# A backward scan of maxima in one instruction, or in pieces of 128 columns

## The chip, the cores and the metric

The kernel runs on one core of a Trainium2 chip. The core has five engines with a queue of instructions each: TensorE (PE in the profile; its weight loads are PEld), VectorE (DVE), ScalarE (ACT), GpSimd (POOL) and SyncE (SP). They work side by side and wait for each other through semaphores, each engine in the order of its own queue. The metric is the device time of one execution in microseconds.

## The reference, cut to what matters

Four graph layers run one after the other over the same graph of 12500 nodes and 212500 edges, sorted by the node that they end in (`dst`): two graph attention layers (GAT), a transformer convolution with 8 heads, a message layer that takes a maximum, and a layer that takes a mean. The first three hold a softmax over the edges of each node. From the transformer convolution:

```python
alpha = jnp.einsum('ehd,ehd->eh', q[dst], k[src]) / jnp.float32(np.sqrt(HD))
m = jax.ops.segment_max(alpha, dst, num_segments=n)
ex = jnp.exp(alpha - m[dst])
den = jax.ops.segment_sum(ex, dst, num_segments=n) + 1e-16
a = ex / den[dst]
agg = jax.ops.segment_sum(a[:, :, None] * v[src], dst, num_segments=n)
```

The GAT layers do the same with one logit for each edge, `leaky_relu(alpha_src[src] + alpha_dst[dst], 0.2)`. What matters here is `m[dst]`: each edge needs the maximum over all edges of its node, in each head.

## The kernel before

The edges lie in chunks of 128, one edge for each partition; a tile is 17 chunks (`U`), and there are 98 tiles (`T`). A layer is a pass over the tiles (`edge_pass`): gat1, gat2, attn, max and sum follow each other. A pass is written out as a calendar of rounds: the parts of a tile's work (`load`, `gather`, `e1`, `chain`, `e2`, `batch`, `ends`) are generators that are put at fixed rounds, and in each round every live generator issues its next few instructions. This settles the order of each engine's queue; nothing reorders it later. Parts of three or four tiles are interleaved.

For a tile, POOL gathers the rows of the source nodes, one indirect DMA for each chunk (L1245), into 17 or 18 buffers of three chunks (`g`). `e1` makes the logits: with matmuls against one-hot matrices (L1528, tile `ex`) in the GAT passes, with L1646, L1651 and L1652 in attn. `chain` makes the maxima and the exponentials. `e2` multiplies the gathered rows with the exponentials (L1580 in the GAT passes, L1675 in attn). That is the last reader of a gather buffer, and POOL's next gather into that buffer waits for it. `batch` sums the products into the nodes of a tile (L1300, one-hot matrix `sef` or `se` from L1291 or L1134), and `ends` finishes the nodes: in attn with a dense network, of which L880 is the last matmul and L713 the statistics on its result.

The maxima are made in `chain` by `node_max`. The logits are transposed (L1463, tile `lt`), so that the edges run along the free axis: one row of 128 columns for each chunk and head. `k` is the number of neighbouring chunks that one row holds one after the other, with one more at each end for the edges that a node has there: k = 1 and 17 rows in the GAT passes, k = 3 and 6 x 8 = 48 rows in attn. The list `n0` holds 0 where an edge has the node of the edge before it and -1e30 where a new node starts. A forward scan (L1451, `fw`) goes through k + 2 chunks: state = max(state + n0, logit). At the last edge of a node it has the node's maximum. A backward scan (L1470, `bw`) over the last k + 1 chunks carries that value back to the node's other edges: 256 columns in the GAT passes, 512 in attn. The forward scan works in stretches of four chunks, since it reads PSUM banks; in attn it is one of 512 columns and one of 128, which starts from the last value of the first. Then PE transposes k chunks of `bw` back (L1475, tile `pbx`), DVE subtracts (L1554 to L1561, or L1664), and ACT takes the exponential (L1563, or L1666). In gat2, DVE's L832 stands between the scan and L1554; SP's store L833 waits for it, and the loads of `n0` (L1415) and `gt` (L1307) come behind that store in SP's queue.

Of the kernel before, what the change touches and what calls it, by code (L numbers as in the profile page):

```python
# [14 lines left out]
ALU = mybir.AluOpType  # L15
# [6 lines left out]
P = 128  # L22
# [43 lines left out]
def gnn_kernel(ctx, tc, a, out):  # L66
    nc = tc.nc
    V, S, GP, PE, SY = nc.vector, nc.scalar, nc.gpsimd, nc.tensor, nc.sync
# [140 lines left out]
    k = WB * P + 1  # L209
    GP.iota(rd_i[0:1, :k], pattern=[[1, k]], base=-k, channel_multiplier=0)  # L210
    k = E - (U * P * (T - 1) - WB * P - 1)
    GP.iota(rd_i[96:, k:], pattern=[[1, EW + 2 - k]], base=4 * NP, channel_multiplier=0)
    GP.memset(dd_i[0:1, 0:1], -1)
    k = E - (P - 1) * RC * P
# [915 lines left out]
    def by4(tag, name):  # L1130
        return psum([P, 512], tag, name).rearrange("p (j e) -> p j e", e=P)
# [309 lines left out]
    def node_max(pool, lg, n0, k, h, pb):  # L1441


        g = -(-U // k)
        r, w = g * h, (k + 2) * P
        fw = pool.tile([r, w], F32, name="fw")
        todo = None

        def forward():
            s0, n, lt = todo  # L1450
            V.tensor_tensor_scan(fw[:, s0 * P:(s0 + n) * P], n0[:, s0 * P:(s0 + n) * P],  # L1451
                                 lt[:r, :n, :].rearrange("p j e -> p (j e)"),
                                 fw[:, s0 * P - 1:s0 * P] if s0 else 0.0,
                                 op0=ALU.add, op1=ALU.max)

        for s0 in range(0, k + 2, 4):
            n = min(4, k + 2 - s0)
            if todo:
                forward()
            lt = by4("pm", "lt")  # L1460
            for s in range(s0, s0 + n):
                g0 = (s - 1) // k + 1
                PE.transpose(lt[:r, s - s0, :],  # L1463
                             lg[:, (s - 1) % k, g0:g0 + g, :].rearrange("p g h -> p (g h)"), ident)
            todo = s0, n, lt
            yield
        forward()
        yield
        bw = pool.tile([r, w - P], F32, name="bw")
        V.tensor_tensor_scan(bw[:, ::-1], n0[:, P + 1:w + 1][:, ::-1], fw[:, P:][:, ::-1], 0.0,  # L1470
                             op0=ALU.add, op1=ALU.max)
        yield
        pb = pb[:, :k * r].rearrange("p (s r) -> p s r", s=k)
        for s in range(k):
            PE.transpose(pb[:, s, :], bw[:, s * P:(s + 1) * P], ident[:r, :r])  # L1475
        yield
        return pb.rearrange("p s (g h) -> p s g h", g=g)
# [11 lines left out]
    class gat(Pass):  # L1489
# [54 lines left out]
        def chain(self, u):  # L1544
            pool, c = self.pool, self.c
            n = chunks_of(u)
            am, lg = self.am[u], self.lg[u]
            neighbours(self.lg, u, 1)
            yield
            ps_ = psum([P, 512], "ex", "pbx")  # L1550
            pb = yield from node_max(pool, lg, self.n0[u], 1, 1, ps_)

            ml = pool.tile([P, 2, U], F32, name="ml")
            V.tensor_tensor(ml[:, 0, :n], am[:, :n, 0], pb[:, 0, :n, 0], ALU.add)  # L1554
            V.tensor_tensor(ml[:, 1, :n], am[:, :n, 0], lg[:, 0, 1:1 + n, 0], ALU.add)
            V.scalar_tensor_tensor(ml[:, :, :n], ml[:, :, :n], 0.2, ml[:, :, :n],
                                   op0=ALU.mult, op1=ALU.max)
            V.tensor_max(ml[:, 0, :n], ml[:, 0, :n], am[:, :n, 1])
            d = pool.tile([P, 2, U], F32, name="d")
            V.tensor_tensor(d[:, 0, :n], ml[:, 1, :n], ml[:, 0, :n], ALU.subtract)  # L1560
            V.tensor_tensor(d[:, 1, :n], am[:, :n, 1], ml[:, 0, :n], ALU.subtract)  # L1561
            p = self.p[u] = ps_[:, 256:256 + 2 * U].rearrange("p (i c) -> p i c", i=2)
            S.activation(p[:, :, :n], d[:, :, :n], AF.Exp)  # L1563
            yield

            lo = self.lo[u] = pool.tile([P, U, 2], F32, name="lo")
            fi = FIRST[:, u * U:u * U + n]
            V.tensor_mul(lo[:, :n, 0], p[:, 1, :n], fi)
            S.copy(lo[:, :n, 1], fi)
            yield  # L1570
# [40 lines left out]
    class attn(Pass):  # L1611
# [43 lines left out]
        def chain(self, u):  # L1655
            pool = self.pool
            lg = self.lg[u]
            neighbours(self.lg, u, 3)
            yield
            ps_ = psum([P, 512], "ex", "pbx")  # L1660
            pb = yield from node_max(pool, lg, self.n0[u], 3, H, ps_)
            g = -(-U // 3)
            d = pool.tile([P, 3, g, H], F32, name="d")
            V.tensor_tensor(d, lg[:, :, 1:g + 1, :], pb, ALU.subtract)  # L1664
            p = self.p[u] = ps_[:, 256:256 + 3 * g * H].rearrange("p (g s h) -> p g s h", s=3, h=H)
            S.activation(p, d.rearrange("p s g h -> p g s h"), AF.Exp)  # L1666
            yield
# [245 lines left out]
```

## Time and profile before

| what | value |
|---|---|
| time, median of 4 runs | 14943.55 us (14927.04 to 14957.47) |
| profiled execution | 14959.69 us, its span 14958.0 us |
| instructions in the profile | 149840 |
| backward scans L1470 | 294: 196 of 17x256, 98 of 48x512 |
| granted TensorE clock, 2000 to 3000 us (gat1) | 0.50 |
| granted TensorE clock, 5200 to 6300 us (gat2) | 0.59 |
| granted TensorE clock, 7300 to 8300 us (attn) | 0.77 |

The profile is one execution on the chip. A line of the timeline has the start and the duration in us, the engine, the line of the kernel, the operation, the tile it writes and those it reads, their shape, and in brackets how long the engine was idle before and what ended that. A line of the groups has the shape, the count, the busy time in us, the mean duration of one in ns and the idle time before them. "Remote" stands for a wait that the profile can't put down to an instruction, "issue" for idle time without such a wait.

### The profile page before, as it was taken

What the parts mean: (1) busy time and instruction counts of PE and PEld (TensorE: products, weight loads), DVE (VectorE), ACT (ScalarE), POOL (GpSimd) and SP (SyncE); (2) the same over time, 40 slices, a digit from 0 to 9 for tenths busy, and PEclk for the clock granted to TensorE, in tenths of its full rate; (3) what the DMA queues carried; (4) which work ended last, traced back from release to release, by engine and by line L of the source; (5) the groups of instructions that cost most, each with busy time, mean ns of one, the idle gap of its engine ahead of it and who ended that gap; (6) DMA issues with size and microseconds to landing.
All of it is one profiled execution on the core that took longest, in us unless ns stands there. A gap on an engine that the chain in (4) does not pass through costs nothing. (4 is left out here: it accounts for less than half of the span.)

```text
span 14958.0 us, 149840 instructions
## 1 busy us (share of the span) xinstructions
PE 7844.6 (52%) x47184; PEld 6088.4 (41%) x47185; DVE 4582.6 (31%) x15188; ACT 4642.6 (31%) x13171; POOL 7855.1 (53%) x8330
## 2 busy tenths in 40 slices
PE   4444444444555555455555555568887785333333
PEld 2222222223444444344444444446665563333333
DVE  4333333332333333344444444423333331000000
ACT  4444444442333333233333333323333332111111
POOL 3445445545555555444444444455555555666665
PEclk5555555555555555677777777767777776666666
DMA  4211111112233322333333333322222222222222
GB/s 112 57 52 50 49 47 50 49 53 80 86 86 86 86 85 85 92 97 97 101 96 97 98 101 97 94 64 75 75 73 75 76 75 59 67 69 70 69 68 68
DMA packets 759391, 1146.93 MB, mean 77 GB/s; under 512 B 224152, under 2 KB 491623, under 8 KB 758479
## 3 DMA queue, kind: packets, MB, share of 16 engines
q0 software_dynamic: 292368, 610.29, 16.0%
q1 hardware_dynamic: 465536, 526.83, 11.1%
q8 instruction: 374, 6.13, 0.2%
q14 instruction: 441, 3.61, 0.1%
q10 hardware_dynamic: 672, 0.07, 0.0%
HBM read 964.76 MB, written 171.69 MB: 76 GB/s over the span
## 5 line engine op out<-in xcount | busy, mean ns | idle before, releaser
L1245 POOL DMA_INDIRECT g<-t,IDX x3322 | 3138.2, 945 | 2947.4 <-issue 1943.9
L1300 PE MATMUL acc<-xf,sef 128*128 128x131 f32 (+2 forms) x13458 | 2752.1, 367 | 1093.5 <-issue 352.5
L1300 PEld LDWEIGHTS acc<-xf,sef 128*128 128x128 f32 x13458 | 2395.2, 263 | 1300.7 <-issue 448.7
L1245 POOL DMA_INDIRECT g<-tkv,IDX x1661 | 1569.7, 945 | 2005.4 <-DVE xf L1675 1490.1
L1245 POOL DMA_INDIRECT g<-ts__84,IDX x1661 | 1567.5, 944 | 1151.6 <-issue 422.2
L1245 POOL DMA_INDIRECT g<-th,IDX x1661 | 1567.8, 944 | 936.7 <-issue 517.7
L1300 PE MATMUL acc<-g,sef 128*128 128x129 f32 x4486 | 883.5, 376 | 1569.8 <-ACT sef L1291 1083.1
L1300 PEld LDWEIGHTS acc<-g,sef 128*128 128x128 f32 x4486 | 818.9, 282 | 1634.4 <-ACT sef L1291 1128.6
L1291 ACT CAST sef<-se 128x512 f32<-128x512 fp8e4 (+1 forms) x1755 | 1030.0, 599 | 1197.0 <-remote 957.0
L1528 PE MATMUL ex<-ADX,st 128*128 128x6 bf16 x4486 | 362.5, 175 | 1216.7 <-ACT st L1134 494.9
L1716 DVE TENSOR_TENSOR_SCAN fm<-n,fm,pg 128x384 f32<-128x384 bf16 (+1 forms) x585 | 567.0, 969 | 1351.9 <-PE pg L1713 557.8
L1315 DVE COPY_PREDICATED r<-FLAG,gt 128x129 f32<-128x129 int32 (+2 forms) x490 | 144.9, 296 | 2568.4 <-ACT r L1321 1913.2
L1528 PEld LDWEIGHTS <-st 128*128 128x128 fp8e4 x4486 | 332.2, 115 | 1436.4 <-issue 747.9
L1651 DVE TENSOR_TENSOR g<-qe,g 128x384 f32<-128x384 f32 x586 | 310.4, 530 | 1601.7 <-remote 1305.5
L1726 ACT COPY xf<-pt_f 128x384 f32<-128x384 f32 x586 | 270.2, 461 | 1271.0 <-PE pt_f L1722 389.2
L1141 PE MATMUL pm_st<-fe,NF 5*128 5x384 bf16 (+2 forms) x877 | 381.5, 458 | 528.8 <-ACT se L1134 477.6
L1646 PE MATMUL qe<-q,st 128*128 128x128 bf16 x6729 | 586.5, 249 | 62.9 <-DVE g L1651 35.8
L1149 PE MATMUL pm_se<-NF,fa 5*128 5x128 bf16 x4486 | 618.8, 278 | 0.0
L1300 PEld LDWEIGHTS <-se 128*128 128x128 fp8e4 x2243 | 238.3, 130 | 910.6 <-issue 555.8
L1134 ACT ACTIVATE se<-pm_se,ones 128x512 fp8e4<-128x512 f32 (+1 forms) x585 | 390.8, 668 | 694.4 <-remote 461.4
L1300 PE MATMUL acc<-xs,se 128*128 128x201 bf16 x2243 | 483.6, 368 | 197.9 <-ACT se L1134 134.7
L1134 ACT ACTIVATE st<-pm_st,ones 128x384 fp8e4<-128x384 f32 (+2 forms) x877 | 468.6, 534 | 365.5 <-PE pm_st L1141 199.6
(1099 smaller groups left out, 12510.7 us busy)
## 6 DMA issues: line engine op xcount, KB each, us to landing
se<-se_d SPq DMA_DIRECT2D x294, 368.0 KB
st<-st_d SPq DMA_DIRECT2D x196, 368.0 KB
g<-t,IDX POOLq DMA_INDIRECT x3322
n<-first_d SPq DMA_DIRECT2D x97, 544.0 KB
st_d<-st SPq DMA_DIRECT2D x98, 368.0 KB
se_d<-se SPq DMA_DIRECT2D x98, 368.0 KB
g<-tkv,IDX POOLq DMA_INDIRECT x1661
g<-ts__84,IDX POOLq DMA_INDIRECT x1661
```

Of the source, the lines that this page charges most:

```text
L1134: S.activation(out, pm[:, :out.shape[1], :], AF.Relu, scale=-1.0, bias=ones[:, 0:1], saturate=False)
L1141: PE.matmul(pm[:, :n, :].rearrange("p j e -> p (j e)"), NF, f[:, c * P:(c + n) * P], start=True, stop=True)
L1149: PE.matmul(pm[:, j, :], f[:, (c + j) * P:(c + j + 1) * P], NF, start=True, stop=True)
L1245: GP.indirect_dma_start(out=g[:, j, :], out_offset=None, in_=self.table, in_offset=bass.IndirectOffsetOnAxis(ap=IDX[:, k:k + 1], axis=0))
L1291: S.copy(se, self.se[t][:, at, :])
L1300: PE.matmul(acc[:, :m], se[:, j, :], x[:, i, :], start=(b == 0 and j == 0), stop=(b == n - 1 and j == len(ws) - 1))
L1315: V.copy_predicated(r[:, :w], FLAG[:, t:t + 1].to_broadcast([P, w]), self.gt[:, :w])
L1528: PE.matmul(ex[:, 6 * k:6 * k + 6], st, ADX[:, t, :, :].rearrange("p s v -> p (s v)"), start=(first and c0 == 0), stop=(stop and c0 + n - ...
L1646: PE.matmul(qe[0][:, k - c0, :], st, self.q[t][:, s * D:(s + 1) * D], start=(first and s == 0), stop=(stop and s == 2))
L1651: V.tensor_mul(k, qe[0][:, :n, :], k)
L1716: V.tensor_tensor_scan(fm[:, :m, :].rearrange("p j e -> p (j e)"), self.n0[u][:, cols], pg, self.prev, op0=ALU.add, op1=ALU.max)
L1726: S.copy(ft[:, :m, :D], pt[:, :m, :])
```

## The change

The backward scan is split into k + 1 instructions of 128 columns each, made from the last chunk to the first. The first of them starts from 0.0 as the whole scan did; each other one starts from the first column of the piece behind it, which is the last value that the backward scan made there, read as a value for each partition. What is computed is the same. There are two instructions in place of one in the GAT passes and four in attn, so 294 scans become 784. The line numbers behind it move by four; the new scan is L1472.

```diff
         bw = pool.tile([r, w - P], F32, name="bw")
-        V.tensor_tensor_scan(bw[:, ::-1], n0[:, P + 1:w + 1][:, ::-1], fw[:, P:][:, ::-1], 0.0,
-                             op0=ALU.add, op1=ALU.max)
+        for s in reversed(range(k + 1)):
+            at = slice(s * P, (s + 1) * P)
+            V.tensor_tensor_scan(bw[:, at][:, ::-1], n0[:, P + 1:][:, at][:, ::-1],
+                                 fw[:, P:][:, at][:, ::-1],
+                                 bw[:, (s + 1) * P:(s + 1) * P + 1] if s < k else 0.0,
+                                 op0=ALU.add, op1=ALU.max)
         yield
```

## The prediction

> **What bounds the kernel now.** I read the engine row of the page first.
>
> ```profile
> PE 7844.6 (52%) x47184; PEld 6088.4 (41%) x47185; DVE 4582.6 (31%) x15188; ACT 4642.6 (31%) x13171; POOL 7855.1 (53%) x8330
> ```
>
> No engine is full, so waits set the time, not work. The change touches DVE only, and DVE is idle for 69% of the span; an average says nothing here. The second view is the groups of instructions with different shapes kept apart, for the backward scan (L1470) and its nearest relative, the forward scan (L1451).
>
> ```profile
> L1451 DVE TENSOR_TENSOR_SCAN fw<-n,lt 17x384 f32<-17x384 bf16 x196 | 184.6, 942 | 718.2 <-PE lt L1463 333.1 <-remote 314.5 <-PE ex L1528 70.5
> L1470 DVE TENSOR_TENSOR_SCAN bw<-n,fw 17x256 f32<-17x256 bf16 x196 | 133.0, 678 | 6.6
> L1470 DVE TENSOR_TENSOR_SCAN bw<-n,fw 48x512 f32<-48x512 bf16 x98 | 119.2, 1217 | 3.3
> L1451 DVE TENSOR_TENSOR_SCAN fw<-n,lt 48x512 f32<-48x512 bf16 x98 | 118.7, 1211 | 140.1 <-PE lt L1463 130.0 <-remote 10.1
> L1451 DVE TENSOR_TENSOR_SCAN fw<-n,fw,lt 48x128 f32<-48x128 bf16 x98 | 45.3, 463 | 0.2 <-PE lt L1463 0.2
> ```
>
> The number after the busy time is the mean of one in ns. The last row is what the change makes: 128 columns that start from a value in SBUF. The third view is the timeline, one tile in each of the three passes that call the scan. Pass gat1 (200 to 3350 us), a tile:
>
> ```profile
> 2038.69 0.94 POOL L1245 DMA_INDIRECT g<-t,IDX  x1 [0.30 <-issue]
> ...
> 2046.07 0.94 DVE L1451 TENSOR_TENSOR_SCAN fw<-n,lt 17x384 f32<-17x384 bf16 x1 [3.55 <-PE lt L1463]
> ...
> 2047.04 0.68 DVE L1470 TENSOR_TENSOR_SCAN bw<-n,fw 17x256 f32<-17x256 bf16 x1
> ...
> 2047.78 0.29 PE L1475 MATMUL pbx<-ident,bw 17*128 17x17 f32 x1
> ...
> 2049.14 0.20 ACT L1563 ACTIVATE pbx<-d 128x34 f32<-128x34 f32 x1 [0.60 <-DVE d L1561]
> ...
> 2049.48 0.37 DVE L1580 TENSOR_TENSOR x<-g,pbx 128x195 f32<-128x195 f32 x1
> ...
> 2050.61 0.94 POOL L1245 DMA_INDIRECT g<-t,IDX  x1 [10.98 <-issue]
> ```
>
> The reader is to see a ring. POOL's last gather of a run starts at 2038.69. The forward scan, the backward scan, the transpose, the exponential and the first product L1580 follow one on the other. L1580 frees a gather buffer, and POOL, idle for 10.98 us, starts again 0.76 us behind its end. Sixteen more gathers at 1.25 us bring the next ring. POOL starts 2.88 to 2.90 us after the end of the backward scan in nearly all tiles of gat1, and the scan starts 8.33 to 8.57 us after POOL's last gather. In gat2 (3350 to 6170 us) the same two distances are 3.08 and about 5.1 us:
>
> ```profile
> 5529.64 0.68 DVE L1470 TENSOR_TENSOR_SCAN bw<-n,fw 17x256 f32<-17x256 bf16 x1
> 5530.25 0.25 DVE L832 TENSOR_TENSOR q__42695<-rest,q__42695 128x128 bf16<-128x128 f32 x1
> ...
> 5530.38 0.28 PE L1475 MATMUL pbx<-ident,bw 17*128 17x17 f32 x1 [5.49 <-DVE bw L1470]
> ...
> 5533.40 0.94 POOL L1245 DMA_INDIRECT g<-t,IDX  x1 [7.84 <-ACT xf L1583]
> ```
>
> In the attention pass (6170 to 9760 us) the ring closes too, at L1675, but PE is not waiting for the scan:
>
> ```profile
> 7530.00 1.22 DVE L1470 TENSOR_TENSOR_SCAN bw<-n,fw 48x512 f32<-48x512 bf16 x1
> ...
> 7531.03 1.16 PE L880 MATMUL p<-w_wf,fT 128*128 128x128 f32 x8
> ...
> 7532.12 0.26 PEld L1475 LDWEIGHTS pbx<-ident,bw 48*128 48x128 f32 x3
> 7532.12 0.38 PE L1475 MATMUL pbx<-ident,bw 48*128 48x48 f32 x3
> 7532.23 0.30 DVE L713 BATCH_NORM_STATS2 st<-p 128x6 f32<-128x128 f32 x1 [1.01 <-PE p L880]
> ```
>
> The scan ends at 7531.22. The transposes stand behind L880 in PE's queue and start at 7532.12, 0.90 us later, and so in every steady tile. In the gat passes they start 0.05 us after the scan. The slack here is therefore 0.85 us.
>
> **The change part by part.**
>
> Removed: 196 scans of 678 ns and 98 of 1217 ns.
>
> Added: two pieces for each of the 196, four for each of the 98. From the two L1470 rows a column costs (1217 - 678)/256 = 2.105 ns and the fixed part is 678 - 256 x 2.105 = 139 ns. The piece that starts from 0.0 is 139 + 128 x 2.105 = 409 ns. A piece that starts from a value in SBUF: 463 ns by the 48x128 row, against 1211 - 384 x 2.105 = 403 for the same without it, so the initial value costs 60 ns. I take 465. Between two pieces lies a wait of DVE on itself. The trace of before has that link between the two scans: forward to backward, 942 ns and a start 0.98 us later, idle 6.6 us / 196 = 34 ns. I take 35.
>
> Gat passes: 409 + 35 + 465 = 909 against 678, +0.231 us a tile. Attention: 409 + 3 x 500 = 1909 against 1217, +0.692 us a tile.
>
> What lies on the path. PE's first transpose (s = 0) reads the piece that is written last, so nothing starts sooner. In gat1 all of the +0.231 is in the ring: the path from the scan's end to POOL's start is serial. 96 tiles have a next one: 96 x 0.231 = 22 us. In gat2 nine tiles have the transpose 0.71 us or more behind the scan, since PE is in an accumulation (L1300); these hide it. 87 x 0.231 = 20 us. In attention the 0.692 fits under L880's 0.85, with 0.16 to spare, and DVE's own next instruction (L713) waits 1.01 us for L880 as well. Only the first two tiles and the last of the pass are open: 3 x 0.69 = 2 us. Sum: +44 us.
>
> Does a ring pass a delay on? The trace holds trials. In gat2, where the transposes came 0.71 late, POOL started 0.71 late and the next backward scan came after 29.5 us instead of 28.84. In gat1 POOL once (scan at 1533.88) started 2.57 us late by itself, and the next scan was 2.2 late. One case speaks against it: at 2686.61 POOL was 0.35 late and the next scan only 0.06.
>
> Queued behind the longer scan: on DVE, in gat2, L832, for which SP's store of q waits (L833), and behind that in SP's queue the load of n0 and gt. n0 is issued at 5502.08 and used at 5528.67, gt is used 5 us after its issue; 0.23 us is covered. POOL's queue and all DMAs keep their order and number. If the cover in attention were gone, each tile would pay what exceeds 0.85 us.
>
> The uncertain price is the link between two pieces. Lower end: nothing for link and initial value, 409 + 409 - 678 = +0.140, or 26 us over the 183 tiles. Upper end: the slowest start behind DVE alone in these rings, POOL's behind L1675, 0.26 us (7535.80 to 7536.06; the 0.76 us behind L1580 holds a wait for ACT as well): 409 + 260 + 465 - 678 = +0.456, so 83 us, and in attention 409 + 3 x 725 - 1217 = +1.367, 0.52 past the cover in 95 tiles, 49 us and 4 for the open ones: 136 us in all. I take 35 ns, since the row is DVE after DVE, on the same tiles. A gain from the pieces themselves is excluded: they hold all the columns of before.
>
> A rule of the Trainium skill stands against this sum. The rows: 139 ns fixed, 60 for the initial value and 35 for the link. The page "Perfetto Trace Analysis", section "Optimizing Scalar/DVE Operations", gives some 60 ns of access time for a DVE instruction on SBUF and says that breaking up instructions may let work finish sooner when a DVE that is not saturated causes bubbles on other engines. By it 183 more instructions would cost 11 us at most, an estimate, and might gain. This trace has 139 + 60 + 35 = 234 ns for one more, and it shows the bubble (PE waits for the scan), but the piece that PE reads first is made last.
>
> **The rivals.**
>
> 1. The attention pass opens. Each link beyond about 0.09 us puts attention on the path as well. For it: the spare is only 0.16 us. Against: 34 ns in the rows. Up to +136 us, 15079.
>
> 2. The ring of gat1 swallows it, as at 2686.61, and only gat2 pays: 20 + 2 = +22 us, 14966. This is no measurable difference; about 0.2%, 30 us, can be told from none.
>
> 3. Faster, by the clock. In gat1 the granted clock is 0.50 throughout, and the matmuls between ACT's release at 2043.29 and the end of the lt transposes at 2046.03 take 2.74 us of the ring. If the shifted rhythm won a full-clock stretch there, as gat2 has one of 3.41 us in each tile, they would halve: -1.37 x 96 = -131 us, with the +44 a net -87, 14857. It decides from 0.77 us a tile on, (44 + 30)/96. Against it: the later scan adds idle time of PE, which makes the matmuls sparser.
>
> **How the numbers follow.** The profiled execution took 14959.69 us (span 14958.0), 16 us above the median of the four runs shown, 14943.55, and 2 above their highest. On its own time the sum gives 15004; the times that count are compared by the median, so 14943.55 + 44 = 14988. Chances: the forecast 0.68, rival 1 0.10, rival 2 0.15, rival 3 0.07. Slower by over 0.2%: 0.78; within: 0.15; faster: 0.07. The range must hold 8 in 10: it takes the forecast, the lower part of rival 1 and the upper part of rival 2, 14957 to 15040.
>
> **What would show it.** L1472 with 196 pieces near 409 ns and 196 near 465 at 17 partitions, 98 and 294 at 48, and 34 ns idle before each; the period in gat1 and gat2 0.23 us longer (about 32.18 and 29.08 us); in attention 36.4 us as before, with the transposes 0.2 us behind the scan instead of 0.90. Wrong: a link of 0.1 us or more, a gat1 period that stays, or a granted clock over 0.50 in gat1.

## The result

| | median | range | runs |
|---|---|---|---|
| before | 14940.73 us | 14919.44 to 14963.93 | 52 |
| changed | 14961.24 us | 14936.37 to 14980.82 | 32 |

The ratio is 1.0013, with a 95% interval of 1.0008 to 1.0017. That is +12 to +25 us, a small loss, clear of none, and below the 0.2% (30 us) that the prediction thought could be told from none. The forecast was +44 us, 14988; the time lies within its range of 14957 to 15040, near the lower end.

### The profile page after: what moved, and what is told of

Its sections match the earlier page's. It is cut to its first block, busy times and chain, and to the rows that moved or that the text cites. A ratio compares the mean times of both kernels' runs of the same rounds, so it can differ in the third digit from the quotient of the medians.

```text
span 14955.4 us, 150329 instructions
## 1 busy us (share of the span) xinstructions
PE 7829.9 (52%) x47184; PEld 6073.4 (41%) x47185; DVE 4689.0 (31%) x15678; ACT 4645.0 (31%) x13171; POOL 7856.3 (53%) x8330
## 5 line engine op out<-in xcount | busy, mean ns | idle before, releaser
L1451 DVE TENSOR_TENSOR_SCAN fw<-n,lt 17x384 f32<-17x384 bf16 (+1 forms) x294 | 303.3, 1032 | 1001.1 <-PE lt L1463 625.6
L1149 PE MATMUL pm_se<-NF,fa 5*128 5x128 bf16 x4486 | 614.5, 277 | 0.0
L1134 ACT ACTIVATE se<-pm_se,ones 128x512 fp8e4<-128x512 f32 (+1 forms) x585 | 391.1, 669 | 664.5 <-remote 484.4
L1134 ACT ACTIVATE st<-pm_st,ones 128x384 fp8e4<-128x384 f32 (+2 forms) x877 | 468.4, 534 | 400.5 <-PE pm_st L1141 169.6
```

The lines of the kernel that those rows point to most:

```text
L1134: S.activation(out, pm[:, :out.shape[1], :], AF.Relu, scale=-1.0, bias=ones[:, 0:1], saturate=False)
L1149: PE.matmul(pm[:, j, :], f[:, (c + j) * P:(c + j + 1) * P], NF, start=True, stop=True)
```

## The profile after

The engine row of the page of the changed kernel:

```profile
PE 7829.9 (52%) x47184; PEld 6073.4 (41%) x47185; DVE 4689.0 (31%) x15678; ACT 4645.0 (31%) x13171; POOL 7856.3 (53%) x8330
```

DVE has 490 instructions and 106 us more; the others have as many instructions as they had, and their busy times differ by 15 us at most. The span is 14955.4 us, 2.6 less than in the profile of before, although the kernel is slower by the timed runs. One pair of spans therefore decides nothing; the passes are compared one by one below.

The groups by shape, forward scan (L1451) and backward pieces (L1472):

```profile
L1451 DVE TENSOR_TENSOR_SCAN fw<-n,lt 17x384 f32<-17x384 bf16 x196 | 184.6, 942 | 863.1 <-PE lt L1463 493.5 <-remote 267.4 <-PE ex L1532 79.4
L1472 DVE TENSOR_TENSOR_SCAN bw<-n,bw,fw 48x128 f32<-48x128 bf16 x294 | 140.0, 476 | 10.4
...
L1472 DVE TENSOR_TENSOR_SCAN bw<-n,bw,fw 17x128 f32<-17x128 bf16 x196 | 92.6, 473 | 7.0
...
L1472 DVE TENSOR_TENSOR_SCAN bw<-n,fw 17x128 f32<-17x128 bf16 x196 | 80.7, 412 | 6.6
...
L1472 DVE TENSOR_TENSOR_SCAN bw<-n,fw 48x128 f32<-48x128 bf16 x98 | 40.8, 416 | 3.3
```

The piece from 0.0 takes 412 to 416 ns and the piece from a value 473 to 476. The idle time between them is 7.0 us / 196 = 36 ns. From the first piece's start to the last one's end a GAT tile takes 0.920 us (0.679 before), an attention tile 1.952 (1.217 before).

The timeline of a tile of gat1, from POOL's last gather of a run to its next start:

```profile
2040.53 0.94 POOL L1245 DMA_INDIRECT g<-t,IDX  x1 [0.30 <-issue]
...
2043.14 0.58 ACT L1134 ACTIVATE st<-pm_st,ones 128x384 fp8e4<-128x384 f32 x1 [2.55 <-remote]
...
2044.71 0.69 ACT L1134 ACTIVATE se<-pm_se,ones 128x512 fp8e4<-128x512 f32 x1 [0.98 <-PE pm_st L1141]
...
2047.63 0.94 DVE L1451 TENSOR_TENSOR_SCAN fw<-n,lt 17x384 f32<-17x384 bf16 x1 [5.32 <-PE lt L1463]
...
2048.61 0.41 DVE L1472 TENSOR_TENSOR_SCAN bw<-n,fw 17x128 f32<-17x128 bf16 x1
...
2049.05 0.47 DVE L1472 TENSOR_TENSOR_SCAN bw<-n,bw,fw 17x128 f32<-17x128 bf16 x1
...
2049.58 0.29 PE L1479 MATMUL pbx<-ident,bw 17*128 17x17 f32 x1 [0.25 <-DVE bw L1472]
...
2051.28 0.37 DVE L1584 TENSOR_TENSOR x<-g,pbx 128x195 f32<-128x195 f32 x1
...
2052.41 0.94 POOL L1245 DMA_INDIRECT g<-t,IDX  x1 [10.95 <-ACT se L1134]
```

The lower half of the ring is as forecast: the scan ends 0.24 us later behind its start, and POOL starts 2.89 us after its end, as before. The upper half is not as before: from POOL's last gather to the scan it is 2048.61 - 2040.53 = 8.08 us here, and was 8.35 in the tile of before. Over the pass the medians are 8.08 and 8.40 us.

A tile of gat2, and one of the attention pass:

```profile
5545.84 0.41 DVE L1472 TENSOR_TENSOR_SCAN bw<-n,fw 17x128 f32<-17x128 bf16 x1
5546.29 0.47 DVE L1472 TENSOR_TENSOR_SCAN bw<-n,bw,fw 17x128 f32<-17x128 bf16 x1
...
5546.81 0.28 PE L1479 MATMUL pbx<-ident,bw 17*128 17x17 f32 x1 [0.16 <-DVE bw L1472]
...
5549.84 0.94 POOL L1245 DMA_INDIRECT g<-t,IDX  x1 [8.16 <-ACT xf L1587]
...
7514.98 0.42 DVE L1472 TENSOR_TENSOR_SCAN bw<-n,fw 48x128 f32<-48x128 bf16 x1
7515.43 1.50 DVE L1472 TENSOR_TENSOR_SCAN bw<-n,bw,fw 48x128 f32<-48x128 bf16 x3
7516.00 1.16 PE L880 MATMUL p<-w_wf,fT 128*128 128x128 f32 x8
7517.09 0.38 PE L1479 MATMUL pbx<-ident,bw 48*128 48x48 f32 x3
7517.20 0.30 DVE L713 BATCH_NORM_STATS2 st<-p 128x6 f32<-128x128 f32 x1 [0.27 <-PE p L880]
```

In gat2 POOL starts 3.08 us after the scan's end (5546.76), as before. In attention the scan ends at 7516.93 and the transposes follow 0.16 us later: still behind L880, and the cover is nearly used up.

The length of each pass, from its first backward scan's start to its last one's, worked out from the start times of these scans in the two timelines:

| pass | before | after | difference | forecast |
|---|---|---|---|---|
| gat1 | 3075.5 us | 3081.4 us | +5.9 | +22 |
| gat2 | 2806.4 us | 2821.5 us | +15.0 | +20 |
| attention | 3487.9 us | 3491.2 us | +3.3 | +2 |

That is +24 us, near the timed +20. Each length is from one profiled execution; in three profiles of the first two groups below that have the whole scan in gat1, its length differed by 2.4 us (3103.4 to 3105.8). The two profiles' spans hide it since the max pass, which the change doesn't touch, was 28 us shorter in the second one (2712.6 and 2684.4 us from its first gather to the next pass's first). Over the eight kernels of the first two groups below, none of which touches it, this pass took 2678.6 to 2710.1 us.

So the miss is in gat1: it should have paid 22 us and paid 6. The trace shows where. Added up over the pass, the scans took 23.4 us more and the stretch from a scan's end to POOL's start 0.6 us more, but the stretch from POOL's last gather to the scan took 19.1 us less. Some 4 us after POOL's last gather, ACT goes on after a wait for PE, and it is not always the same instruction that goes on. I took for each tile the ACT instruction that starts 3.5 to 4.5 us after the last gather and had waited over 0.7 us. Of 92 tiles, in the profile of before it was L1134 on `st` in 56 (7.41 us from the last gather to the forward scan, period 31.92) and L772 in 24 (7.56, 32.07). After the change it was L1134 on `se`, a later step of the same work, in 53 (7.08, 31.83), `st` in 14 (7.42, 32.17) and L772 in 14 (7.71, 32.47). Where the step is the same, the period grew: by 0.25 us with `st`, as forecast, and by 0.40 us with L772. Where ACT was one step further, 0.33 us was won back. In the profile of before only five tiles were of the `se` kind, and two of them come next after the two late starts of POOL that the prediction names (scans at 1533.88 and 2686.61): there too a later start of the gathers went with one more step (a third late start, by 0.3 us behind the scan at 381.29, did not). From this comes theory A of the experiments: PE's signals to ACT come late while POOL gathers, and the number of steps that get through before the last gather moves the ring by more than the change does.

## The experiments

They were made in four groups, each on one chip. The kernel before took 15035 us in the first, 15029 in the second, 10767 in the third and 10762 in the fourth, against 14941 above. Ratios are to the kernel before of the same group.

### One pass at a time

The diff, with `size` from the caller: 256 or 512 leaves the scan whole, 128 makes pieces. Three kernels have pieces in one pass each.

```diff
-        V.tensor_tensor_scan(bw[:, ::-1], n0[:, P + 1:w + 1][:, ::-1], fw[:, P:][:, ::-1], 0.0,
-                             op0=ALU.add, op1=ALU.max)
+        for e in range(w - P, 0, -size):
+            at = slice(e - size, e)
+            V.tensor_tensor_scan(bw[:, at][:, ::-1], n0[:, P + 1:][:, at][:, ::-1],
+                                 fw[:, P:][:, at][:, ::-1],
+                                 bw[:, e:e + 1] if e < w - P else 0.0,
+                                 op0=ALU.add, op1=ALU.max)
```

> Pieces of 128 columns in the first GAT pass alone, the whole scan elsewhere. Theory A (read from the two traces): the scan ends 0.24 us later in each tile, but the stretch from POOL's last gather to the backward scan gets shorter in most tiles (8.40 to 8.08 us), because work of PE and ACT that does not wait for the scan gets 0.24 us more before POOL's next gathers hold up the handing on from PE to ACT. Then the pass grows by 0 to 10 us (period 32.00 to about 32.05 on the mean) and the whole by as much. Theory B (the sum of the prediction): the ring pays every tile, 96 x 0.231 = +22 us, period +0.23, and the short stretch in the profile of the changed kernel was chance.

> Pieces in the second GAT pass alone. Theory A: here the stretch from POOL's last gather to the scan stays at 5.0 to 5.1 us, so the pass pays nearly all: +15 to +20 us, period 28.96 to about 29.13. Theory B: +20 us. A third theory, that the whole +20 us of the change comes from several places in equal parts: +10 us.

> Pieces in the attention pass alone, four for each tile. Both theories: the transposes start about 0.17 us behind the scan instead of 0.90, the period stays at 36.43, the pass grows by 0 to 4 us (edge tiles). Rival: the loss of the spare 0.73 us shows up elsewhere, +10 us or more.

| pieces in | ratio | that is | the pass, against whole in the other two kernels |
|---|---|---|---|
| gat1 | 1.0030 (1.0018 to 1.0041) | +45 us | 3142.4 against 3105.3: +37 |
| gat2 | 1.0007 (0.9998 to 1.0016) | +11 us | 2885.9 against 2869.5: +16 |
| attention | 1.0002 (0.9993 to 1.0011) | +3 us | 3502.1 against 3502.3: 0 |

The timed intervals of gat2 and attention hold no change as well; the lengths of their passes fit theory A (+15 to +20, and 0 to +4). In this group PE was in an accumulation in more tiles of gat2: with the whole scan the transposes came 0.8 us late in 37 and 39 of 98 tiles (9 in the profile of before), and these hide the delay. Some 60 x 0.241 = 14 us is left, an estimate.

Theory A's number for gat1 (0 to 10 us) is wrong on this chip, and theory B's +22 is too low. A tile of gat1 with pieces there, with PE's L1149 early in the run of gathers and ACT's L1134 that waits for it:

```profile
2069.87 0.60 PE L1149 MATMUL pm_se<-NF,fa 5*128 5x128 bf16 x4
...
2080.60 0.69 ACT L1134 ACTIVATE se<-pm_se,ones 128x512 fp8e4<-128x512 f32 x1 [9.92 <-remote]
2080.69 0.94 POOL L1245 DMA_INDIRECT g<-t,IDX  x1 [0.30 <-issue]
...
2083.40 0.58 ACT L1134 ACTIVATE st<-pm_st,ones 128x384 fp8e4<-128x384 f32 x1 [1.95 <-remote]
...
2084.83 0.27 ACT L772 COPY gr<-pm 128x128 f32<-128x128 f32 x1 [0.85 <-PE pm_se L1149]
```

ACT goes on 10.1 us after PE's matmuls ended (2070.47), while POOL gathers. The profile models the ends of matmuls; whether the matmuls or only their signal came late it can't tell, and "late signal" stands for both here. 4.1 us after the last gather it has come only to L772, in 66 of 92 tiles, and in 75 of 92 with the whole scan (the kernel with pieces in attention alone). No step is won here; the stretch from the last gather to the forward scan even grows, from 7.72 to 7.83 us in these tiles, and the period from 32.26 to 32.62. So gat1 swallowed most of the delay on one chip and added to it on another.

### The gathers of gat1 as plain transfers

```diff
             for j in range(n):
                 k = u * U + c + j
+                if isinstance(self, gat) and not self.made:
+                    GP.dma_start(out=g[:, j, :], in_=self.table[rows((7 * k) % (T - 1)), :])
+                    continue
                 GP.indirect_dma_start(
```

> The kernel before, but in the first GAT pass POOL's queue issues a plain transfer of 128 neighbouring rows of the table in place of each gather by indices, so the rows are not those of the edges' source nodes. Everything else stays, POOL's waits for free buffers too. Theory A: the 3.5 to 5.5 us that ACT sits idle behind PE's L1149, L1141 and L769 while POOL gathers go away (below 0.5 us each), the stretch from the last transfer to the scan shrinks from 8.4 to under 3 us, and the pass gets at least a third shorter (3075 us to under 2100). Rival: the idle times of ACT are not POOL's doing (order of ACT's queue, or the clock): they stay, and the pass shrinks only by what POOL's issue takes less.

13912 us in its one run, 1123 less. What ACT's L1134 waited for in gat1 (us, times), first in the kernel with whole scans there and gathers (pieces in attention alone), then with plain transfers:

```profile
  remote: 829.8, 126
  PE pm_st L1141: 176.6, 139
  issue: 153.4, 21
  PE pm_se L1149: 113.7, 192
```

```profile
  PE pm_se L1149: 185.4, 285
  PE pm_st L1141: 123.8, 96
```

The late signals are gone: with plain transfers each of these L1134 that had waited starts 0.04 us after PE's matmul ended, at the most. The period, from two scans of neighbouring tiles:

```profile
1201.76 0.68 DVE L1473 TENSOR_TENSOR_SCAN bw<-n,fw 17x256 f32<-17x256 bf16 x1
...
1222.12 0.68 DVE L1473 TENSOR_TENSOR_SCAN bw<-n,fw 17x256 f32<-17x256 bf16 x1
```

20.36 us in place of 32.3, and the pass 2003.5 us in place of 3105: more than the third that theory A asked for. The run shows that PE's signals are late on this chip when POOL gathers by indices and prompt when it issues plain transfers. It doesn't show what the lateness costs. POOL's issue takes 537 ns in place of 947 for one transfer, and from the first transfer of a run to the last it is 10.7 us in place of 20.0 (medians): 9.3 of the 11.9 us that the period lost. The stretch from the last transfer to the scan, for which theory A expected under 3 us, is still 6.30 us, against 8.69 with gathers. So late signals are not all of this stretch, and the rival, that POOL's faster issue shortens the pass, holds for most of the gain as far as the period goes. Its other half, that ACT's waits stay, does not hold.

### The whole change on this kind of chip

> The change as it is, on the chip of this group. If the three passes add up as on the chip of the single-pass runs: first GAT pass +20 to +40 us where its stretch from the last gather to the scan is 8.7 us in the kernel before, 0 to +10 us where it is 8.4 us; second GAT pass +13 to +20; attention 0 to +4. Theory A: the first GAT pass is the one that differs from chip to chip. Theory B: +20 us in the first GAT pass on every chip.

1.0037 (1.0022 to 1.0051): +56 us. gat1 3141.4 us against 3103.5 whole (the kernel with 64 columns in attention), +38; gat2 2883.6 against 2871.3, +12; attention 3500.3 against 3497.9 (the kernel with a delay), +2. The stretch from the last gather to the scan is 8.69 us in this group's kernel with 64 columns in attention, and theory A's range for 8.7 us held; the range came from the run before and doesn't say why. Theory B's +20 did not hold. That the first pass alone differs much from chip to chip holds: +6 there, +37 and +38 here.

### Twice as many pieces in attention

`size` is 64 in attention and whole elsewhere.

> Pieces of 64 columns in the attention pass alone, eight for each tile, the GAT passes as before. A tile's scan should take 1217 + 7 x 234 = 2.85 us, 1.64 more than whole; the cover under L880 is 0.85 us. If the cover is what hides the change in attention, 0.79 us a tile shows, up to 95 x 0.79 = +75 us, and the transposes start 0.05 us behind the scan. Rival (the attention pass keeps its own rhythm, for instance with the clock): less than +20 us.

1.0059 (1.0042 to 1.0076): +89 us; the pass takes 3589.6 us, 92 more.

```profile
7512.29 0.28 DVE L1472 TENSOR_TENSOR_SCAN bw<-n,fw 48x64 f32<-48x64 bf16 x1
7512.61 2.61 DVE L1472 TENSOR_TENSOR_SCAN bw<-n,bw,fw 48x64 f32<-48x64 bf16 x7
7513.32 1.16 PE L880 MATMUL p<-w_wf,fT 128*128 128x128 f32 x8
...
7515.27 0.38 PE L1479 MATMUL pbx<-ident,bw 48*128 48x48 f32 x3 [0.80 <-DVE bw L1472]
```

L880 is done 0.74 us before the scan is, and PE waits; the transposes start 0.05 us behind the scan, as expected. The scan takes 2.93 us, 1.71 more than whole; less the cover of 0.85 that is 0.86 x 95 = 82 us, and 3 open tiles make 5 more. The loss has the size that the cover leaves over, and the rival's limit of 20 us is passed: the cover hid the change's four pieces.

### A delay of another kind

```diff
+        for n in delay:
+            V.tensor_tensor_scan(pool.tile([r, w], F32, name="dly")[:, :n], n0[:, :n], fw[:, :n], 0.0,
+                                 op0=ALU.add, op1=ALU.max)
         bw = pool.tile([r, w - P], F32, name="bw")
```

> The scan whole, with one needless scan of 128 columns ahead of it in both GAT passes (its result is not read): +0.44 us a tile, twice the change's +0.24. If rings pass a delay on in full: 97 x 0.44 = +43 us in each pass. Theory A (steps in the handing on while POOL gathers): the first GAT pass differs from that by up to 0.4 us a tile in either direction; the second stays near +0.3 to +0.44.

```profile
2022.21 0.94 DVE L1451 TENSOR_TENSOR_SCAN fw<-n,lt 17x384 f32<-17x384 bf16 x1 [1.61 <-PE lt L1463]
2023.19 0.41 DVE L1470 TENSOR_TENSOR_SCAN dly<-n,fw 17x128 f32<-17x128 bf16 x1
2023.53 0.65 DVE L1473 TENSOR_TENSOR_SCAN bw<-n,fw 17x256 f32<-17x256 bf16 x1
```

The delay came out smaller than I had worked out: the needless scan takes 0.41 us, but the next one doesn't read it and starts 0.34 after its start, so a tile is 0.315 us later and not 0.44. 1.0032 (1.0019 to 1.0046), +48 us. gat1 took 3141.4 us, the same as with the change's 0.24; gat2 2898.1, +27 or 0.28 a tile. In gat1 two different delays thus cost the same, 37 to 38 us; in proportion they would have been 23 and 31.

`delay` is one scan of 128 columns here, in the GAT passes alone. Two further kernels, one with two memsets (the diff) and one with two needless scans, were to give more points of that line, but they came to a chip of the other kind:

```diff
+        if k == 1:
+            for _ in range(2):
+                V.memset(pool.tile([r, 1], F32, name="dly"), 0.0)
         bw = pool.tile([r, w - P], F32, name="bw")
```

> The scan whole, two needless memsets of one column ahead of it in both GAT passes: some 0.1 us a tile. So far, on this group's kind of chip, the first GAT pass (first to last backward scan) took 3104 to 3106 us whole and with 0.40 us less of scans, and 3141 to 3142 us with 0.24 and with 0.32 us more. Theory A (steps): it takes one of two values, about 3105 or about 3141, not one between. Theory B (in proportion): 3105 + 10 to 16 us. The second GAT pass 2870 + 6 us by either.

> The scan whole, two needless scans of 128 columns ahead of it in both GAT passes: +0.32 us for the first by the run with one, +0.44 for the second, +0.76 in all. Theory A (steps): the first GAT pass stays at the step of 3141 us or jumps to a next one 35 to 70 us above; it is not at 3105 + 97 x 0.76 = 3179 within 5 us. Theory B: 3179 us. Second GAT pass: 2870 + 97 x 0.76 = 2944 us by proportion, 2920 to 2944 expected.

The memsets gave no delay at all: they ran before the forward scan ended, and the backward scan started 0.976 us behind the start of the forward one, as ever. So this kernel shows the one before, 1.0001 (0.9991 to 1.0011), on a chip where it takes 10767 us. The profile of it, what L1134 waited for in gat1, and some lines of a run of gathers:

```profile
  PE pm_se L1149: 179.3, 278
  PE pm_st L1141: 117.6, 93
```

```profile
1508.60 0.94 POOL L1245 DMA_INDIRECT g<-t,IDX  x1 [0.30 <-issue]
...
1509.14 0.60 PE L1149 MATMUL pm_se<-NF,fa 5*128 5x128 bf16 x4
...
1509.85 0.69 ACT L1134 ACTIVATE se<-pm_se,ones 128x512 fp8e4<-128x512 f32 x1
1509.85 0.94 POOL L1245 DMA_INDIRECT g<-t,IDX  x1 [0.30 <-ACT xs L1485]
```

POOL gathers, and ACT follows PE 0.11 us behind (1509.74 to 1509.85). No late signal is left in this pass, POOL hardly stops, and the passes are POOL's: 17 x 1.249 = 21.2 us a tile (2062.7 us for gat1, 2056.2 for gat2, 2091.3 for attention). With two needless scans (0.63 us a tile) gat1 took 2064.2 us, gat2 2067.6: 1.0008 (0.9998 to 1.0018), +9 us (-2 to +19) of the 122 that a ring would pass on. With the same gathers, 1.249 us apart, and prompt signals gat1 takes 2063 us here and 3105 on the slower kind of chip; this is the nearest that the runs come to a price of the late signals, and it compares two chips, not one cause. Whether gat1's cost goes in steps could not be settled: neither theory's line was measured at other points on the slower kind of chip.

### Narrower scans

Both scans take 64 columns of a neighbouring chunk in place of 128, and the test that puts a tile with a longer node on the list for a separate treatment looks 64 edges ahead in place of 128. A node of more than 64 edges now goes the way that one of more than 128 went before.

```diff
+M = 64
...
-        eq = wp.tile([T, EW - P], BF16, name="eq")
+        eq = wp.tile([T, EW - M], BF16, name="eq")
-        V.scalar_tensor_tensor(eq, w[:, P:], 0.0, w[:, :EW - P], op0=ALU.add, op1=ALU.is_equal,
+        V.scalar_tensor_tensor(eq, w[:, M:], 0.0, w[:, :EW - M], op0=ALU.add, op1=ALU.is_equal,
...
-            V.tensor_tensor_scan(fw[:, s0 * P:(s0 + n) * P], n0[:, s0 * P:(s0 + n) * P],
+            a, e = max(s0 * P, P - M), min((s0 + n) * P, w - P + M)
+            V.tensor_tensor_scan(fw[:, a:e], n0[:, a:e],
...
+        e = w - 2 * P + M
+        V.tensor_tensor_scan(bw[:, :e][:, ::-1], n0[:, P + 1:P + 1 + e][:, ::-1],
+                             fw[:, P:P + e][:, ::-1], 0.0, op0=ALU.add, op1=ALU.max)
```

> Both scans over less: 64 columns of each neighbouring chunk in place of 128, and nodes of more than 64 edges are put on the list of nodes that are made separately (before: over 128), which leaves the list as it is for these inputs. Forward scan in the GAT passes 256 columns in place of 384 (678 ns in place of 942), backward scan 192 in place of 256 (543 in place of 678): -0.40 us a tile. Ring passes it on in full: -39 us in each GAT pass, -78 in all. With the second GAT pass at 0.7 of it and the first at anything between 0 and 1.3: -25 to -80 us.

0.9981 (0.9971 to 0.9991): -28 us, on a chip of the second group.

```profile
L1453 DVE TENSOR_TENSOR_SCAN fw<-n,lt 17x256 f32<-17x256 bf16 x196 | 131.9, 673 | 452.2 <-PE lt L1464 216.3 <-remote 176.7 <-issue 34.4
L1472 DVE TENSOR_TENSOR_SCAN bw<-n,fw 17x192 f32<-17x192 bf16 x196 | 106.9, 545 | 6.6
```

The 0.40 us are there, 942 - 673 and 679 - 545. gat1 gained nothing from them (3106.0 against 3103.5 us), gat2 16 us of 39 (2855.2 against 2871.3), and attention, where I had expected none, 10 (3487.6 against 3497.9); the cause of the last I don't know.

### More buffers for the gathers of gat1

```diff
             self.c, self.w, self.source, self.made = c, c + 3, source, source is not None
+            self.bufs = 18 if self.made else 24
```

> The whole scan, and 24 buffers for gathered rows in the first GAT pass in place of 18 (18 in the second as before), so that POOL need not wait for the first product of a tile. If the ring (scan, exponential, product, buffer, gathers) sets the first pass: its period falls from 32.3 us towards POOL's own 17 x 1.25 = 21.3 us. Theory A adds that PE's signals stay late while POOL gathers without a break, so that the pass falls by less, to a period of 25 to 31 us. Rival: the ring is not what sets the pass, and the period stays at 32.3.

This ran in the third group, so it tells nothing of the ring with late signals. 0.9986 (0.9976 to 0.9995), -14 us; gat1 2048.4 us against 2062.7.

> The narrower scans of the run with 64 columns and the 24 gather buffers of the first GAT pass together. Where POOL gathers without a break and PE's signals are prompt (the kernel before near 10767 us): the buffers alone gave -14 us; the narrower scans lie beside the gathers and add 0 to -15 us. Where PE's signals come late while POOL gathers (the kernel before near 14940 or 15030 us): the narrower scans give -28 us; if the buffers let POOL go on without waiting for the first product, the first pass either falls (period under 32) or, since PE's signals are then late throughout, stays or grows. Sum for that case: 14900 to 15060 us.

0.9968 (0.9956 to 0.9980), -35 us (-47 to -22) where -14 to -29 was expected, in the fourth group: gat1 2037.6 us, gat2 2056.3, attention 2082.4. It beats the kernel before on the faster kind of chip; the changed kernel was not run there, and this one was not run on the slower kind.

## Why the prediction was right, and where it was not

The direction was right and the time lies in the range, but only because the range took in the upper part of rival 2: the forecast itself was twice what came. A loss of over 0.2% had a chance of 0.78 and did not come, and one of the prediction's own signs of being wrong did, "a gat1 period that stays" (median 31.95 us before, 31.86 after).

- **The price of the pieces.** Forecast 409 and 465 ns and a link of 34 to 35 ns; measured 412 to 416, 473 to 476 and 36. +0.241 us a GAT tile against +0.231, +0.735 an attention tile against +0.692. Right.
- **"In gat1 all of the +0.231 is in the ring: the path from the scan's end to POOL's start is serial. 96 x 0.231 = 22 us".** This is the step that failed. The path named is serial and did not change (2.89 us), but the ring has another half, which I took as fixed: from POOL's last gather to the scan. It went from 8.40 to 8.08 us (medians), and the pass paid 5.9 us. On the chips of the first two groups the same half grew (8.69 to 8.81 and 8.85), and the pass paid 37 and 38 us. That PE's signals come late in the run of gathers is shown, and that they are prompt with plain transfers; that run leaves 6.30 of the 8.69 us of this half, so the late signals are at most a part of it. Why a scan that ends 0.24 us later lets one more step through on one chip and not on another was not shown. A reason that fits the first is that PE and ACT have 0.24 us more for work that doesn't wait for the scan before POOL starts; it is argued only.
- **gat2.** 87 x 0.231 = 20 us forecast, 15.0 measured, 16 and 12 in the groups. The steady tile pays what was forecast (median period 28.86 to 29.11), and POOL's start stays at 3.08 us. The nine tiles of before with a late transpose became five, with 0.5 us in place of 0.8. In the groups more tiles hid the delay (37 to 42 of 98 with the whole scan).
- **Attention.** +2 us forecast, +3.3 measured, 0 and +2 in the groups. The transposes came 0.16 us behind the scan (0.2 forecast), and the run with 64 columns shows that the cover ends where the prediction put it.
- **The sum.** +44 us forecast, +20 measured, since gat1 left out 16 and gat2 5 of it. In the second group the same kernel lost 56 us: gat1 paid 16 more than forecast there, by way of the same half of the ring.
- **The rivals.** Rival 2, that gat1's ring swallows it, gave the price (+22) and the place. The single tile at 2686.61 that I gave for it, where a delay vanished before the next scan, was no exception: after the change most tiles were of its kind, with ACT at `se`. The link stayed short, so attention did not open; the granted clock in gat1 stayed at 0.50 (between 1000 and 3000 us), so the third rival fell too. That the whole came so near to rival 2's +22 is in part luck: gat1 paid 6 where it has nothing, and gat2 15 where it has 20.
- **The Trainium skill's rule.** "Perfetto Trace Analysis", "Optimizing Scalar/DVE Operations", has some 60 ns of access time for a DVE instruction on SBUF, and I set 234 ns for one more against it. Both sizes occur here. A needless scan that nothing reads adds 0.315 us, 46 ns more than its 128 columns (269 ns); a piece that the next one reads adds 0.241 us for no more columns. The page's figure is near the first and far from the second. The section adds that the latency of an instruction in a profile is about twice its figure, which the prediction's 11 us at most left out; twice 60 ns is still half of the 241. That smaller instructions may let work finish sooner, as the section says, no run here shows.

## What to carry to other kernels

Where a ring of waits sets the time, look at all of it: a delay that is passed on in full on one side can be won back or added to on the other, if that side holds waits that the profile can't put down to an instruction ("remote"). One more instruction in a chain on DVE cost 241 ns here, five times the 46 ns that one beside the chain cost over its columns. Small changes to such a kernel should be measured on more than one chip, and pass by pass: here the same edit cost 20 us on one chip and 56 on another.

## What was not expected of the hardware

- While POOL gathers by indices, the signal that PE's matmuls are done reached ACT up to 10 us late in gat1 (2070.47 to 2080.60 in the lines above). With plain transfers from POOL's queue on the same chip it took 0.04 us.
- This is not so on every chip. The kernel before took 14941, 15035 and 15029 us in three sets of runs and 10767 and 10762 in two others. In the profile of the faster kind the gathers come at the same 1.249 us, a gather takes the same 0.94 to 0.95 us, the granted clock in gat1 is the same 0.50, and L1134 starts 0.1 us after PE's end at the most where it had waited in gat1. What sets the chips apart no run here shows.
- Two DVE scans that don't depend on each other overlap: the second started 0.34 us after the start of one of 0.41 us. Where the second reads the first, it started 36 ns after the first one's end.
